# Small comparisons and sums moved from VectorE to GpSimd in an attention kernel, and one early projection moved to another bank

## The chip, the cores and the metric

One core of one Trainium2 chip. The metric is the device time of one execution in microseconds (us), the median of the runs. Below, TensorE is also PE, VectorE is DVE, ScalarE is ACT, GpSimd is POOL, and SyncE, which here only issues transfers, is SP, as in the profile. PEld is TensorE's weight load.

## The reference

The input `x` is 32 images of 256 channels and 32 x 32 pixels, all float32. Each image goes through a group normalisation, 1x1 projections to queries, keys and values (8 heads of 32), causal attention in which a pixel sees only earlier ones, and a residual sum:

```
x = x + conv(_gn(x))
_gn:   g = v.reshape(B, 32, 8, H, W); (g - mean(g)) / sqrt(var(g) + 1e-5)
conv:  q = q_w @ xf + q_b;  k, v = split(kv_w @ xf + kv_b)          # xf: (B, 256, 1024)
       scores = q @ k^T / sqrt(32), masked to tril(-1)
       attn = softmax(scores), 0 where masked;  out = attn @ v
```

## The kernel before

**Visits.** An image is worked through in ten visits: two groups of four heads, five visits each (`VISITS`, lines 638 to 650). In each visit TensorE writes scores of keys against queries, the long pieces into the banks `sT` and the short ones into `tri`; ScalarE takes exponentials without a maximum, of `sT` into `e` (L443, two a visit) and of `tri` into `eh` (L446, three buffers that take turns by visit, line 416); GpSimd sets the masked half of the diagonal blocks to zero (L388, `select`, called by `mask`). One visit later TensorE multiplies the exponentials with the values into the bank `acc` (L472), and VectorE adds the exponentials of different keys up (L490, `add_keys`) for the softmax's denominators.

**Order of the work.** The schedule is written out by hand: nothing is reordered, so that each engine's queue runs in the order in which the loop at line 820 emits. In each turn of that loop the order is: the scores of visit i with their exponentials and selections, the first half of the products of visit i - 1, the list `at[i]`, the second half of those products, `add_keys` of visit i - 1, the list `after[i]`. Work that belongs to other images is hung on visits through `when`: the tuples at lines 720 to 726 (`PROJECT`, `PREPARE`, `SUMS`, `STACK`, `LOAD`, `SPREAD`, `FINISH`) say on which visit, counted from the image's own first visit.

**Normalisation of an image**, eleven to twelve visits ahead of it (`PREPARE`): VectorE's statistics per channel (L196), a transfer out and an indirect transfer back that brings the eight channels of a group together (L205, L212, the latter issued by GpSimd), `norm_groups` (line 217): VectorE aggregates them to mean and variance (L219, twice), and with two small operations on 128x2 numbers makes minus the mean (L222) and the variance plus 1e-5 (L224). One visit later `norm_rstd` (line 248) on GpSimd: the power -0.5 (L250), and `shift`, the product of minus the mean and that (L254). One visit later again, `norm_apply` on ScalarE makes the normalised input `xn` from `x`, `shift` and `rstd` (L269), four operations for each of two halves. Image 0 has its own way through `norm_mean` to `norm_variance`, and its `norm_rstd` does the power alone.

**Denominators.** GpSimd issues transfers that fold the sums over 128 partitions to 32 (L505, `fold`, two a row of sums, each with an accumulation), SP stacks the four rows (L511), and in the next image's visits 5 and 6 VectorE transposes and reduces them (L518, L519, `sum_folded`) into `rows`, 128x64. In visit 7 `invert` (line 550) checks that all sums lie between 1e-20 and 1e20: `check` (line 546) multiplies the tile `in_range` with two comparisons (L547, L548). Then come reciprocal (L554), transpose (L556), a transfer out to DRAM (L559), and transfers back that spread the inverses (L573). `finish` on VectorE multiplies and adds the residual (L598, L601, L606). `in_range` is read once, at the end (line 623), where it decides whether a slower way is taken after all.

**Projections.** `project_qk` (line 271) and `project_v` (line 287) are hung on visits by `PROJECT`. Each writes into a bank that is either `room`, half of one of the `sT` tiles (two projections of the same turn get the two halves of one tile), or `lone`, the bank `acc` of the values' products. For image 0 the first ones run before visit 0: queries of the first half in `lone`, keys of the first half in `room`, the first values `v(0)` in the other half of that tile. ScalarE copies each out (L283, L300). `lone` is used again in visit 0, for the queries of the second half.

## Time and profile before

| | |
|---|---|
| median of 3 runs | 1806.36 us (1802.93 to 1806.63) |
| the profiled execution | 1806.47 us, span 1803.3 us, TensorE's granted clock 0.999 |
| GpSimd's busiest lines | selections L388, transfers L505 |
| chain that ended last | PE 57%, DVE 32%, issue 5%, DMA 3%, ACT 2% |
| in that chain by line | additions L490 20%, products L472 17%, projections L180 14 and 7% |
| TensorE's granted clock | full in all 40 slices |

The busy shares of the page count an engine as busy while an instruction is in flight on it, also when that instruction is stretched by another engine; for TensorE, whose matmuls overlap, a busy engine is not one at its peak. So the share alone does not tell which engine sets the pace. Rows of waits are "engine, line, what it waited for: us in total, times, longest"; rows of a timeline are "start, duration, engine, line, operation, output and inputs, shape, count", with the idle time before in brackets and what ended it. The name in front of the arrow is the tile that is written.

### The profile page before, as it was taken

What the parts mean: (1) busy time and instruction counts of PE and PEld (TensorE: products, weight loads), DVE (VectorE), ACT (ScalarE), POOL (GpSimd) and SP (SyncE); (2) the same over time, 40 slices, a digit from 0 to 9 for tenths busy, and PEclk for the clock granted to TensorE, in tenths of its full rate; (3) what the DMA queues carried; (4) which work ended last, traced back from release to release, by engine and by line L of the source; (5) the groups of instructions that cost most, each with busy time, mean ns of one, the idle gap of its engine ahead of it and who ended that gap; (6) DMA issues with size and microseconds to landing.
All of it is one profiled execution on the core that took longest, in us unless ns stands there. A gap on an engine that the chain in (4) does not pass through costs nothing.

```text
span 1803.3 us, 82014 instructions
## 1 busy us (share of the span) xinstructions
PE 1782.8 (99%) x37208; PEld 983.7 (55%) x37208; DVE 1682.6 (93%) x1852; ACT 1469.8 (82%) x1736; POOL 833.2 (46%) x935
## 2 busy tenths in 40 slices
PE   8999999999999999999999999999999999999998
PEld 5555555555555555555555555555555555555554
DVE  3789999999999999999999999999999999999996
ACT  5888888888888888888888888888888888888884
POOL 2445644444444444544544444545444444445541
PEclk9999999999999999999999999999999999999999
DMA  2566776666766767767667666676676676666662
GB/s 69 105 118 129 150 134 137 137 138 136 149 127 138 144 134 148 129 134 143 131 145 146 129 137 142 137 148 128 136 147 131 145 143 131 138 140 136 131 120 86
DMA packets 92771, 240.23 MB, mean 133 GB/s; under 512 B 26272, under 2 KB 27792, under 8 KB 76544
## 3 DMA queue, kind: packets, MB, share of 16 engines
q0 software_dynamic: 17360, 100.58, 39.0%
q1 hardware_dynamic: 74912, 134.28, 26.3%
q8 instruction: 292, 4.78, 1.1%
q14 instruction: 63, 0.52, 0.1%
q10 hardware_dynamic: 144, 0.07, 0.0%
HBM read 69.90 MB, written 34.95 MB: 58 GB/s over the span
## 4 chain that ended last, share of the span: by engine, by line
PE 57%; DVE 32%; issue 5%; DMA 3%; ACT 2%; DVEq 0%; SPq 0%; POOL 0%; ACTq 0%
DVE e L490 20%; PE acc L472 17%; PE pp L180 14%; PE tri L381 10%; PE sT L381 8%; PE ppv L180 7%; DVE turned L518 3%; DVE rows L519 3%; DVE rb L601 2%; DMA rb<-inverses 2%; DVE num L598 2%; ACT eh L446 2%; DVE st L196 1%; PE pd L526 1%; DVE mv L219 1%
## 5 line engine op out<-in xcount | busy, mean ns | idle before, releaser
L443 ACT ACTIVATE e<-sT 128x1024 f32<-128x1024 f32 x640 | 620.8, 1022 | 209.1 <-PE sT L381 204.3
L381 PE MATMUL tri<-q,k 32*64 32x128 f32 (+4 forms) x12416 | 550.4, 298 | 8.8 <-ACT eh L446 8.1
L381 PE MATMUL sT<-q,k 32*64 32x256 f32 (+1 forms) x7424 | 548.7, 462 | 1.2 <-issue 1.2
L381 PEld LDWEIGHTS tri<-q,k 32*64 32x64 f32 x12416 | 389.0, 131 | 185.9 <-issue 86.6
L388 POOL TENSOR_SCALAR_AFFINE_SELECT diagonal<-eh 128x512 f32<-128x512 f32 x384 | 363.2, 966 | 265.6 <-ACT eh L446 265.3
L180 PE MATMUL pp<-xn,wT 128*32 128x512 f32 (+1 forms) x4224 | 477.5, 582 | 0.0
L490 DVE TENSOR_TENSOR e<-e,eh 128x1536 f32<-128x1536 f32 x375 | 438.3, 1169 | 41.5 <-PE acc L472 28.2
L446 ACT ACTIVATE eh<-tri 128x1536 f32<-128x1536 f32 (+1 forms) x320 | 453.2, 1416 | 23.6 <-DVE e L490 23.6
L490 DVE TENSOR_TENSOR e<-e,e 128x2048 f32<-128x2048 f32 x187 | 447.4, 2393 | 6.4
L505 POOL DMA_DIRECT2D e<-e x248 | 206.5, 833 | 414.9 <-DMA e<-e 360.9
L472 PE MATMUL acc<-e,v 128*32 128x512 f32 x2560 | 338.5, 600 | 1.1 <-POOL diagonal L388 1.1
L381 PEld LDWEIGHTS sT<-q,k 32*64 32x64 f32 x7424 | 301.1, 131 | 15.2 <-issue 1.9
L180 PEld LDWEIGHTS pp<-xn,wT 128*32 128x32 f32 x4224 | 140.5, 109 | 270.6 <-issue 216.2
L490 DVE TENSOR_TENSOR e<-e,diagonal 128x1024 f32<-128x1024 f32 x187 | 245.0, 1310 | 19.4
L180 PE MATMUL ppv<-wT,xn 128*32 128x256 f32 x4032 | 240.6, 379 | 0.0
L472 PE MATMUL acc<-eh,v 128*32 128x384 f32 (+3 forms) x3072 | 198.7, 346 | 0.0
L472 PEld LDWEIGHTS acc<-eh,v 128*32 128x32 f32 x3072 | 97.0, 110 | 143.1 <-issue 120.6
L180 PEld LDWEIGHTS ppv<-wT,xn 128*32 128x32 f32 x4032 | 129.7, 110 | 69.0
L388 POOL TENSOR_SCALAR_AFFINE_SELECT e<-e 128x512 f32<-128x512 f32 x64 | 73.2, 1144 | 196.1 <-ACT e L443 196.1
L269 ACT ACTIVATE xn<-x,shift,rstd 128x256 f32<-128x256 f32 x248 | 135.4, 594 | 8.8 <-POOL shift L254 8.4
L601 DVE SCALAR_TENSOR_TENSOR rb<-num,v_bias_col,x 128x256 f32<-128x256 f32 x248 | 131.3, 569 | 4.4
L472 PEld LDWEIGHTS acc<-e,v 128*32 128x32 f32 x2560 | 62.8, 108 | 105.2 <-issue 94.6
(94 smaller groups left out, 1267.9 us busy)
## 6 DMA issues: line engine op xcount, KB each, us to landing
e<-e POOLq DMA_DIRECT2D x124, 512.0 KB, 6.2
x<-in_x_dram SPq DMA_DIRECT2D x124, 256.0 KB, 4.1
e<-e POOLq DMA_DIRECT2D x124, 256.0 KB, 4.7
folded<-e SPq DMA_DIRECT2D x124, 256.0 KB, 4.5
rb<-inverses SPq DMA_DIRECT2D x124, 256.0 KB, 5.0
out_dram<-rb SPq DMA_DIRECT2D x124, 256.0 KB, 3.8
x<-in_x_dram SPq DMA_DIRECT2D x2, 512.0 KB, 5.8
inverses<-inv_turned SPq DMA_DIRECT2D x31, 32.0 KB, 2.9
```

What stands on the lines that cost most here:

```text
L180: nc.tensor.matmul(out[part, cols], lhsT=lhsT[:, part], rhs=rhs[:, cols], start=start, stop=stop, skip_group_check=True)
L269: nc.scalar.activation(to, of, AF.Identity, bias=live["shift", b][:, g : g + 1], scale=rstd)
L381: return nc.tensor.matmul(to[c : c + KEYS, at : at + width], lhsT=live["k", b, g][rows, kb * P + c : kb * P + c + KEYS], rhs=live["q", b, ...
L388: nc.gpsimd.affine_select(out=to, in_=of, pattern=[[0, 4], [(1, -1)[odd], P]], compare_op=ALU.is_gt, fill=0.0, base=0, channel_multiplier= ...
L443: nc.scalar.activation(e[:, heads[a][0] : heads[a][1] + 1 : step, :], banks[a], AF.Exp)
L446: exp = nc.scalar.activation(eh[:, :, :wide], tri.rearrange("p (j q) -> p j q", q=SHORT)[:, :, :wide], AF.Exp)
L472: nc.tensor.matmul(acc[HD * j : HD * (j + 1), of], lhsT=live["v", b][:, kb, h * HD : (h + 1) * HD], rhs=e[:, j, :], start=first, stop=last ...
L490: nc.vector.tensor_add(to, to, tile_of(b, g, at))
L505: nc.gpsimd.dma_start(out=total[:rows], in_=total[rows : 2 * rows], accum_op=ALU.add)
L518: nc.vector.transpose(turned, live["folded", b][:, j, :])
L519: nc.vector.tensor_reduce(live["rows", b][:, j * HALF // HD : (j + 1) * HALF // HD], turned.rearrange("p (k r) -> p k r", r=HD), AX.X, ALU ...
L601: nc.vector.scalar_tensor_tensor(blocks(rb, s), blocks(num, s, (start + s) % 2 == 1), v_bias_col[:, g : g + 1], blocks(xt[:, g, cols], s), ...
```

## The change

- `norm_groups` ends with the two aggregates; L222 and L224 are gone from VectorE.
- `norm_rstd` on GpSimd, for images 1 to 31, does four operations on 128x2 numbers in place of two: variance plus a tile of 1e-5, power, mean times a tile of -1, that times the power. The two constant tiles are set once at the start.
- `check` runs on GpSimd: each of the two comparisons is a `tensor_scalar` into a tile `held`, and a product of `in_range` with it. It is emitted where it was, ahead of the reciprocal in `invert`.
- For image 0, `v(0)` is put into `lone` instead of `room`.

```diff
+    minus = const.tile([P, NG], F32, name="minus")
+    nc.gpsimd.memset(minus, -1.0)
+    least_variance = const.tile([P, NG], F32, name="least_variance")
+    nc.gpsimd.memset(least_variance, 1e-5)
...
         def norm_groups(b):
             for g in range(NG):
                 nc.vector.bn_aggr(live["mv", b][:, g, :], live["eight", b][:, :, g, :])
-            mv = live["mv", b]
-            live["minus_mean", b] = small.tile([P, NG], F32, tag="mean", name=f"mean_{b}")
-            nc.vector.tensor_scalar(live["minus_mean", b], mv[:, :, 0], -1.0, None, ALU.mult)
-            live["rstd", b] = small.tile([P, NG], F32, tag="rstd", name=f"rstd_{b}")
-            nc.vector.tensor_scalar(live["rstd", b], mv[:, :, 1], 1e-5, None, ALU.add)
...
         def norm_rstd(b):
-            rstd = live["rstd", b]
+            if b == 0:
+                nc.gpsimd.tensor_tensor(live["rstd", b], live["rstd", b], power, ALU.pow)
+                return
+            mv = live["mv", b]
+            rstd = live["rstd", b] = small.tile([P, NG], F32, tag="rstd", name=f"rstd_{b}")
+            shift = live["shift", b] = small.tile([P, NG], F32, tag="shift", name=f"shift_{b}")
+            nc.gpsimd.tensor_tensor(rstd, mv[:, :, 1], least_variance, ALU.add)
             nc.gpsimd.tensor_tensor(rstd, rstd, power, ALU.pow)
-            if b == 0:
-                return
-            live["shift", b] = small.tile([P, NG], F32, tag="shift", name=f"shift_{b}")
-            nc.gpsimd.tensor_tensor(live["shift", b], live["minus_mean", b], rstd, ALU.mult)
+            nc.gpsimd.tensor_tensor(shift, mv[:, :, 0], minus, ALU.mult)
+            nc.gpsimd.tensor_tensor(shift, shift, rstd, ALU.mult)
...
-                qk(0, 0, 0, *early), qk(1, 0, 0), qk(0, 0, 1, *early), v(0), qk(1, 0, 1), qk(0, 1, 0, lone),
+                qk(0, 0, 0, *early), qk(1, 0, 0), qk(0, 0, 1, *early), v(0, *early), qk(1, 0, 1), qk(0, 1, 0, lone),
...
-        def check(rows, least, most):
-            nc.vector.scalar_tensor_tensor(in_range, rows, least, in_range, ALU.is_ge, ALU.mult)
-            nc.vector.scalar_tensor_tensor(in_range, rows, most, in_range, ALU.is_le, ALU.mult)
+        def check(b):
+            for n, (bound, order) in enumerate(((SUM_MIN, ALU.is_ge), (SUM_MAX, ALU.is_le))):
+                held = small.tile([P, ROW], F32, tag="held", name=f"held_{b}_{n}")
+                nc.gpsimd.tensor_scalar(held, live["rows", b], bound, None, order)
+                nc.gpsimd.tensor_tensor(in_range, in_range, held, ALU.mult)
...
-            check(rows, SUM_MIN, SUM_MAX)
+            check(b)
```

## The prediction

> **What bounds the kernel now.** I read the page's busy shares first, then who waited for whom on VectorE (DVE) and on TensorE (PE) over a long steady stretch, then both timelines. The page:
>
> ```profile
> PE 1782.8 (99%) x37208; PEld 983.7 (55%) x37208; DVE 1682.6 (93%) x1852; ACT 1469.8 (82%) x1736; POOL 833.2 (46%) x935
> ```
>
> That reads as a TensorE kernel. The waits from 300 to 1690 us say otherwise. First all those of VectorE, then all those of TensorE:
>
> ```profile
> DVE e L490 <- DVE e L490: 0.5, 1, 0.5
> DVE e L490 <- ACT num L481: 0.5, 1, 0.5
> DVE e L490 <- issue: 0.3, 1, 0.3
> ```
>
> ```profile
> PE tri L381 <- ACT eh L446: 6.6, 15, 0.8
> ```
>
> In 1390 us VectorE waited 1.3 us: it always has something ready. TensorE shows more waiting, and all of it on ScalarE's (ACT's) exponential of the short scores. How much TensorE really loses shows in the time from one image to the next. Visit 5 of images 2, 3 and 30 begins on TensorE at (start, duration, engine, line, shapes):
>
> ```profile
> 159.00 0.56 PE L381 MATMUL tri<-q,k 32*64 32x128 f32 x6
> ```
>
> ```profile
> 213.49 0.56 PE L381 MATMUL tri<-q,k 32*64 32x128 f32 x6
> ```
>
> ```profile
> 1705.54 0.56 PE L381 MATMUL tri<-q,k 32*64 32x128 f32 x6
> ```
>
> Image 2 took 213.49 - 159.00 = 54.49 us; the 27 after it took (1705.54 - 213.49) / 27 = 55.26 us each, with the same matmuls. So 54.49 is TensorE's own pace, 0.77 us an image is lost to something else, and over 27 images that is 20.8 us: the most a relief of VectorE can give in the steady part. A busy TensorE hides it, because a held-up visit also runs its matmuls less tightly.
>
> Where the loss is made, on VectorE's and ScalarE's timelines near the end of image 15:
>
> ```profile
> 894.29 0.69 DVE L519 TENSOR_REDUCE rows<-turned 128x16 f32<-128x512 f32 x1
> 895.01 0.23 DVE L547 SCALAR_TENSOR_TENSOR in_range<-rows,in_range 128x64 f32<-128x64 f32 x1
> 895.27 0.23 DVE L548 SCALAR_TENSOR_TENSOR in_range<-rows,in_range 128x64 f32<-128x64 f32 x1
> 895.41 0.55 DVE L554 RECIPROCAL inv<-rows 128x64 f32<-128x64 f32 x1
> ```
>
> ```profile
> 898.02 1.45 ACT L446 ACTIVATE eh<-tri 128x1536 f32<-128x1536 f32 x1 [0.84 <-DVE e L490]
> ```
>
> After four transposes and four reductions comes the inversion, and behind it, late, the additions of L490 that must free a buffer of `eh`. ScalarE stands 0.84 us for it, and the next visit of TensorE for ScalarE. VectorE, late by up to three buffers, is the bound; TensorE stands 0.77 us an image below it. I argue from VectorE's work per image.
>
> **The change, part by part.** *The check leaves VectorE.* From the start of L547 to that of L554 are 895.41 - 895.01 = 0.40 us, and the sums are there (L519 ends 894.98): 0.40 us an image, right ahead of the additions that ScalarE waits for.
>
> *The two small operations after the aggregate leave VectorE.* Image 16, then image 30:
>
> ```profile
> 921.62 0.62 DVE L222 TENSOR_SCALAR mean<-mv 128x2 f32<-128x2 f32 x1
> 922.14 0.15 DVE L224 TENSOR_SCALAR rstd<-mv 128x2 f32<-128x2 f32 x1
> 922.21 3.00 DVE L490 TENSOR_TENSOR e<-e,eh 128x1536 f32<-128x1536 f32 x2
> ```
>
> ```profile
> 1694.64 0.17 DVE L222 TENSOR_SCALAR mean<-mv 128x2 f32<-128x2 f32 x1
> 1694.72 0.16 DVE L224 TENSOR_SCALAR rstd<-mv 128x2 f32<-128x2 f32 x1
> 1694.85 3.17 DVE L490 TENSOR_TENSOR e<-e,eh 128x1536 f32<-128x1536 f32 x2
> ```
>
> ```profile
> L222 DVE TENSOR_SCALAR mean<-mv x31: 168/295/632, 23.9 to 1694.6; 128x2 f32<-128x2 f32 x31
> ```
>
> They take 922.21 - 921.62 = 0.59 us in one image and 0.21 in the other. The rest, 0.38 us, I read as waiting for GpSimd (POOL), whose mask selections run in the first case; the next addition would meet the same selection, so that part comes back in some measure. I credit 0.28 us, near the lower end with the median of 295 ns in view; the ends are 0.21 and 0.38. Both edits: 0.68 us an image.
>
> *What GpSimd's new work costs VectorE.* Six instructions an image are new on GpSimd: two comparisons and two products of 128x64, an addition and a product of 128x2. The page's groups have one comparison of that size (row L620, its mean in ns), and the trace two cases of GpSimd beside VectorE: the power (alone at 8.90, beside VectorE at 925.57) and the selections of 128x512.
>
> ```profile
> L620 POOL TENSOR_SCALAR rows_last<-inv_last 128x64 f32<-128x64 f32 x1 | 0.4, 403 | 9.8 <-DVE inv_last L587 9.8
> ```
>
> ```profile
> 8.90 0.73 POOL L250 TENSOR_TENSOR rstd<-rstd,power 128x2 f32<-128x2 f32 x1 [6.33 <-DVE rstd L246]
> ```
>
> ```profile
> 925.57 1.56 POOL L250 TENSOR_TENSOR rstd<-rstd,power 128x2 f32<-128x2 f32 x1
> 927.21 0.20 POOL L254 TENSOR_TENSOR shift<-mean,rstd 128x2 f32<-128x2 f32 x1
> ```
>
> ```profile
> 926.45 0.68 DVE L598 TENSOR_TENSOR num<-num,rb 128x512 f32<-128x512 f32 x1
> ```
>
> ```profile
> 1788.50 0.67 DVE L598 TENSOR_TENSOR num<-num,rb 128x512 f32<-128x512 f32 x1
> ```
>
> ```profile
> 898.37 0.80 POOL L505 DMA_DIRECT2D e<-e  x1 [3.46 <-DMA e<-e]
> 899.56 2.29 POOL L388 TENSOR_SCALAR_AFFINE_SELECT diagonal<-eh 128x512 f32<-128x512 f32 x2 [0.39 <-ACT eh L446]
> ```
>
> ```profile
> 901.39 2.60 DVE L490 TENSOR_TENSOR e<-e,e 128x2048 f32<-128x2048 f32 x1
> ```
>
> ```profile
> 929.79 2.29 DVE L490 TENSOR_TENSOR e<-e,e 128x2048 f32<-128x2048 f32 x1
> ```
>
> The power is stretched from 0.73 to 1.56 us and ends with VectorE's product (927.13), which lost 0.01 (0.68 against 0.67). A tiny GpSimd instruction yields. A selection does not: the addition beside it lost 2.60 - 2.29 = 0.31 us. So six instructions cost VectorE between 6 x 0.01 = 0.06 us and, the four larger ones at 0.31 x 0.40 / 1.15 (two selections in 2.29 us) = 0.11 each, 0.45 us. I take 0.1: they are nearer in size to the power, and the first two of the check lie beside the reciprocal and a transpose, which read one operand. Net 0.58 us, so VectorE asks for 55.26 - 0.58 = 54.68 us an image, still 0.19 above TensorE.
>
> [...]
>
> *GpSimd's queue.* The check sits behind visit 7's selections and waits in order for the sums (894.98); four instructions of some 0.4 us end about 896.6. Behind it stands the accumulating transfer that went at 898.37 after 3.46 us of idleness, on another transfer. So it is covered by 1.8 us; uncovered, it would push that transfer and the selections of visit 8.
>
> *The longer chain to the normalised input.* Addition, power and two products now run in turn where power and product did, so `shift` comes later by at least two small instructions (0.4 us), by more if each yields to VectorE. ScalarE already waits for it. Visit 4 and 5 on TensorE with the wait in ScalarE's row, image 16 then image 29:
>
> ```profile
> 927.08 0.56 PE L381 MATMUL tri<-q,k 32*64 32x128 f32 x6
> ```
>
> ```profile
> 927.44 1.09 ACT L269 ACTIVATE xn<-x,shift,rstd 128x256 f32<-128x256 f32 x2 [0.40 <-POOL shift L254]
> ```
>
> ```profile
> 932.36 0.56 PE L381 MATMUL tri<-q,k 32*64 32x128 f32 x6
> ```
>
> ```profile
> 1644.79 0.57 PE L381 MATMUL tri<-q,k 32*64 32x128 f32 x8
> ```
>
> ```profile
> 1646.00 1.09 ACT L269 ACTIVATE xn<-x,shift,rstd 128x256 f32<-128x256 f32 x2 [1.25 <-POOL shift L254]
> ```
>
> ```profile
> 1650.53 0.56 PE L381 MATMUL tri<-q,k 32*64 32x128 f32 x6
> ```
>
> Normalising 0.36 us after the visit's start cost nothing (5.28 us to visit 5); 1.21 after cost 0.46 (5.74). So about 0.4 us of slack is left, and `shift` moves 0.4 to 1.3 us. But the chain's place follows VectorE, which arrives 0.40 + 0.28 us earlier: I book 0, with 0.46 as the other end.
>
> *The first value projection.* It stands at the start, once:
>
> ```profile
> 13.50 0.69 ACT L283 ACTIVATE q<-pp,qk_bias 128x512 f32<-128x512 f32 x1 [1.31 <-PE pp L180]
> 15.21 0.69 ACT L283 ACTIVATE k<-pp,qk_bias 128x512 f32<-128x512 f32 x1 [1.03 <-PE pp L180]
> ```
>
> ```profile
> 15.96 1.93 PE L180 MATMUL pp<-wT,xn 128*32 128x256 f32 x32 [0.80 <-ACT k L283]
> ```
>
> It shares a tile with the key projection and waits 0.80 us for that to be copied out. The values' bank is free since 14.19: 0.8 us gained. The ends are 0 (the start waits for a transfer instead) and 0.8. The two new memsets are hidden ahead of the first load.
>
> **The sum.** 27 x 0.58 = 15.7 us, 0.8 at the start, and 1.0 because VectorE, nearly on TensorE's pace, needs some five more images to fall three buffers behind (5 x 0.19): 17.5 us. The profiled execution took 1806.47 us (span 1803.3), 0.1 over the median of the runs: 1806.47 - 17.5 = 1789.0.
>
> **The rivals.**
> - *TensorE's floor.* The additions meet fewer selections once VectorE is less late, and VectorE drops below 54.49: 20.8 + 0.8 gives 1784.9. For it: the gap is only 0.19. Against: GpSimd has more to do.
> - *`shift` becomes the wait.* If every image pays what image 29 paid, the pace is 54.49 + 0.46 = 54.95: 27 x 0.31 + 0.8 = 9.2 us, 1797.3. For it: ScalarE waits here already. Against: VectorE's head start.
> - *GpSimd takes back what VectorE gave.* At 0.45 us for the new work the net is 0.23 an image: 27 x 0.23 + 0.8 = 7.0 us, 1799.5; at 0.6 no change shows.
> [...]
> - *No relief.* VectorE loses the instructions but waits elsewhere: 1806. Its 1.3 us of waits speak against it.
>
> **Chances.** Forecast 0.52, TensorE's floor 0.18, `shift` 0.14, given back 0.07, no relief 0.03, slower 0.06. Within 0.2% (3.6 us, about what three runs spread over and can tell from no change) lie the last part of "given back" and "no relief": 0.07; slower 0.06; faster 0.87. The range goes from TensorE's floor less the spread of the runs, 1783, to 1800, which takes in `shift`.
>
> **What would show it.** Right: VectorE has four instructions fewer an image; images are 54.5 to 54.8 us apart on TensorE; ScalarE's wait for L490 before `eh` mostly gone; the key-copy wait of 0.80 gone; the check ends before the accumulating transfer. Wrong: the mean durations of L490 rise, ScalarE's wait for `shift` grows several-fold with TensorE waiting behind it, or images stay at 55.2.

## The result and the profile after

The changed kernel took 1857.66 us (median of six runs, 1846.47 to 1865.86), the kernel before 1804.79 on the same chip (1802.93 to 1806.63): ratio 1.0286, interval 1.0242 to 1.0331. The forecast was 1789.0 with 1783 to 1800 as its range, so it was wrong, sign included. The profiled execution took 1853.35 us, span 1850.5, 47.2 us longer than before's span.

Line numbers have moved by three to five: scores are L384, exponentials L446 and L449, additions L493; the four operations to `shift` are L254 to L257, the check L552 and L553, the normalisation L272. The page's busy shares:

```profile
PE 1791.7 (97%) x37208; PEld 988.1 (53%) x37208; DVE 1676.7 (91%) x1728; ACT 1463.4 (79%) x1736; POOL 1021.8 (55%) x1123
```

VectorE has its 124 instructions fewer and is no longer the engine that always has work. Over the same stretch as before, 300 to 1690 us, its longest sum of waits, and TensorE's:

```profile
DVE e L493 <- PE acc L475: 24.4, 15, 3.4
```

```profile
PE ppv L184 <- ACT e L446: 40.7, 20, 3.0
```

VectorE's waits of this stretch were 1.3 us in all before, and TensorE had no such wait. Behind it, on ScalarE, over the whole span:

```profile
ACT xn L272 <- POOL shift L257: 71.9, 27, 4.4
```

That wait was 8.4 us before. Visit 5 of images 15, 16 and 17 begins at:

```profile
901.52 0.56 PE L384 MATMUL tri<-q,k 32*64 32x128 f32 x6
```

```profile
960.44 0.57 PE L384 MATMUL tri<-q,k 32*64 32x128 f32 x6
```

```profile
1014.92 0.56 PE L384 MATMUL tri<-q,k 32*64 32x128 f32 x6
```

One image took 58.92 us, the next 54.48. So the pace of 54.49 that the forecast read as TensorE's own is reached, but only in some images. Image 16, at its visit 4, on GpSimd, VectorE, ScalarE and TensorE in turn:

```profile
949.97 0.69 POOL L254 TENSOR_TENSOR rstd<-mv,least_variance 128x2 f32<-128x2 f32 x1
950.74 0.87 POOL L255 TENSOR_TENSOR rstd<-rstd,power 128x2 f32<-128x2 f32 x1
951.59 0.41 POOL L256 TENSOR_TENSOR shift<-mv,minus 128x2 f32<-128x2 f32 x1
952.08 2.25 POOL L257 TENSOR_TENSOR shift<-shift,rstd 128x2 f32<-128x2 f32 x1
```

```profile
951.00 0.95 DVE L493 TENSOR_TENSOR e<-e,eh 128x768 f32<-128x768 f32 x1
951.99 2.29 DVE L493 TENSOR_TENSOR e<-e,e 128x2048 f32<-128x2048 f32 x1
```

```profile
954.37 1.09 ACT L272 ACTIVATE xn<-x,shift,rstd 128x256 f32<-128x256 f32 x2 [3.44 <-POOL shift L257]
955.36 1.91 ACT L446 ACTIVATE e<-sT 128x1024 f32<-128x1024 f32 x2
```

```profile
956.41 3.54 PE L184 MATMUL ppv<-wT,xn 128*32 128x256 f32 x32 [2.37 <-ACT e L446]
```

Read it from the bottom. TensorE stands 2.37 us for visit 4's exponentials; these are queued on ScalarE behind the normalisation, which stands 3.44 us for `shift`; and `shift` is late because a product of two numbers per partition took 2.25 us. It began 0.09 us after VectorE's addition of 128x2048 and ended 0.05 us after it (952.08 + 2.25 = 954.33 against 951.99 + 2.29 = 954.28). Of the 31 products L257 in the trace, the first two, at the start, take 0.20 and 0.19 us; each of the other 29 ends within 0.08 us behind the end of a VectorE instruction that was running, and 13 of them take 2.25 us, beside that same addition. Where VectorE is idle, in image 0, the four take:

```profile
36.98 0.19 POOL L254 TENSOR_TENSOR rstd<-mv,least_variance 128x2 f32<-128x2 f32 x1
37.25 0.72 POOL L255 TENSOR_TENSOR rstd<-rstd,power 128x2 f32<-128x2 f32 x1
37.96 0.18 POOL L256 TENSOR_TENSOR shift<-mv,minus 128x2 f32<-128x2 f32 x1
38.23 0.20 POOL L257 TENSOR_TENSOR shift<-shift,rstd 128x2 f32<-128x2 f32 x1
```

1.45 us from first to last (38.43 - 36.98); in image 16 it is 4.36. The means of the page's groups (last number ahead of the bar's idle time, in ns), with the check's:

```profile
L552 POOL TENSOR_SCALAR held<-rows 128x64 f32<-128x64 f32 x62 | 57.9, 933 | 2.1
L553 POOL TENSOR_TENSOR in_range<-in_range,held 128x64 f32<-128x64 f32 x62 | 54.7, 883 | 5.2
L257 POOL TENSOR_TENSOR shift<-shift,rstd 128x2 f32<-128x2 f32 x31 | 41.7, 1344 | 2.4
L255 POOL TENSOR_TENSOR rstd<-rstd,power 128x2 f32<-128x2 f32 x31 | 33.4, 1078 | 2.4
```

The power L255 takes 1078 ns in the mean (0.72 us in image 0) and the product L257 1344 (0.20), while the additions of 128x2048 beside the 13 products of 2.25 us take 2.29 each, as in image 16. That is the direction that the forecast did not price: here GpSimd is the one that stands.

The stall costs more than the wait. In the stretches from 954 to 956, 956 to 960 and 960 to 964 us (the clock that TensorE was granted is the last number but two):

```profile
954.00:956.00 2.00, 0.04 (x4) 0.00 (x0) 1.96 (x4) 1.63 (x3) 2.00 (x3) 1.00 0.46 130
956.00:960.00 4.00, 3.58 (x44) 1.79 (x48) 3.83 (x5) 2.61 (x3) 0.98 (x2) 0.57 0.95 199
960.00:964.00 4.00, 4.00 (x84) 2.17 (x76) 3.86 (x3) 3.57 (x6) 0.00 (x0) 1.00 0.55 163
```

From 956.32 us, 0.09 us ahead of the end of the idle time, TensorE is granted 0.50 of its clock for 3.41 us (0.50 in the stretch from 956.40 to 959.70), and the projection takes 3.54 us where it takes 1.93 in the prediction's row of the same 32 matmuls. That happened in eight images, for 3.41 us in each.

What a late `shift` costs can be read image by image. Where the first normalisation begins up to 0.54 us behind visit 4's start on TensorE, visit 4 takes its shortest time, 5.28 us. From 1.52 us on it loses that delay less 0.8 us (1.52 gives 0.71, 2.05 gives 1.24, 4.07 gives 3.25), and 1.0 to 1.7 us more in the eight images with half clock: in image 16 a delay of 3.41 us (954.37 against 950.96) costs 4.20.

**Where the 47.2 us are.** I take the start of each visit on TensorE and the shortest time of each of the ten visits in images 2 to 30 as its floor. Image 0 begins 1.28 us earlier (16.54 against 17.82), images 0 and 1 are together 1.13 shorter, images 2 to 30 together 49.6 longer. Within these 49.6: visit 4 lost 62.8 us over its floor (2.4 before), visit 1 6.4 (0.65), visit 5 1.6 (0.03), while the loss in visits 8 and 9 went from 18.2 to 0.1. The ten floors add up to 54.48 us before and 54.47 after.

### The profile page after: what moved, and what is told of

It is laid out like the page before. It is cut to its first block, busy times and chain, and to the rows that moved or that the text cites. A ratio compares the mean times of both kernels' runs of the same rounds, so it can differ in the third digit from the quotient of the medians.

```text
span 1850.5 us, 82078 instructions
## 1 busy us (share of the span) xinstructions
PE 1791.7 (97%) x37208; PEld 988.1 (53%) x37208; DVE 1676.7 (91%) x1728; ACT 1463.4 (79%) x1736; POOL 1021.8 (55%) x1123
## 4 chain that ended last, share of the span: by engine, by line
PE 56%; DVE 15%; POOL 9%; issue 7%; DMA 6%; ACT 5%; POOLq 1%; DVEq 0%; ACTq 0%; SPq 0%
PE acc L475 16%; PE pp L184 15%; DVE e L493 9%; PE tri L384 8%; PE ppv L184 8%; PE sT L384 8%; DMA e<-e 3%; POOL diagonal L391 3%; ACT e L446 2%; DMA eight<-each,group_of 2%; DVE num L603 2%; DVE rb L606 2%; POOL held L552 1%; ACT xn L272 1%; ACT eh L449 1%
## 5 line engine op out<-in xcount | busy, mean ns | idle before, releaser
L446 ACT ACTIVATE e<-sT 128x1024 f32<-128x1024 f32 x640 | 620.1, 1021 | 228.7 <-PE sT L384 215.9
L384 PE MATMUL sT<-q,k 32*64 32x256 f32 (+1 forms) x7424 | 549.1, 462 | 0.5 <-issue 0.5
L384 PE MATMUL tri<-q,k 32*64 32x128 f32 (+4 forms) x12416 | 542.2, 298 | 0.9 <-ACT eh L449 0.9
L493 DVE TENSOR_TENSOR e<-e,eh 128x1536 f32<-128x1536 f32 x375 | 431.9, 1152 | 69.1 <-PE acc L475 55.7
L391 POOL TENSOR_SCALAR_AFFINE_SELECT diagonal<-eh 128x512 f32<-128x512 f32 x384 | 353.8, 958 | 245.1 <-ACT eh L449 244.8
L384 PEld LDWEIGHTS tri<-q,k 32*64 32x64 f32 x12416 | 388.2, 131 | 173.7 <-issue 77.0
L493 DVE TENSOR_TENSOR e<-e,e 128x2048 f32<-128x2048 f32 x187 | 456.5, 2441 | 6.4
L449 ACT ACTIVATE eh<-tri 128x1536 f32<-128x1536 f32 (+1 forms) x320 | 453.0, 1416 | 0.0
L508 POOL DMA_DIRECT2D e<-e x248 | 216.7, 874 | 347.1 <-DMA e<-e 236.2
L384 PEld LDWEIGHTS sT<-q,k 32*64 32x64 f32 x7424 | 302.2, 131 | 14.0 <-issue 1.6
L184 PE MATMUL ppv<-wT,xn 128*32 128x256 f32 x4064 | 252.9, 391 | 44.1 <-ACT e L446 44.1
L493 DVE TENSOR_TENSOR e<-e,diagonal 128x1024 f32<-128x1024 f32 x187 | 250.3, 1339 | 19.4
L272 ACT ACTIVATE xn<-x,shift,rstd 128x256 f32<-128x256 f32 x248 | 135.6, 597 | 72.0 <-POOL shift L257 71.9
L391 POOL TENSOR_SCALAR_AFFINE_SELECT e<-e 128x512 f32<-128x512 f32 x64 | 79.5, 1242 | 178.0 <-ACT e L446 178.0
L606 DVE SCALAR_TENSOR_TENSOR rb<-num,v_bias_col,x 128x256 f32<-128x256 f32 x248 | 135.1, 585 | 4.4
L603 DVE TENSOR_TENSOR num<-num,rb 128x512 f32<-128x512 f32 x124 | 102.5, 827 | 25.0 <-DMA rb<-inverses 22.9
```

The costliest lines, as they stand in the source:

```text
L184: nc.tensor.matmul(out[part, cols], lhsT=lhsT[:, part], rhs=rhs[:, cols], start=start, stop=stop, skip_group_check=True)
L272: nc.scalar.activation(to, of, AF.Identity, bias=live["shift", b][:, g : g + 1], scale=rstd)
L384: return nc.tensor.matmul(to[c : c + KEYS, at : at + width], lhsT=live["k", b, g][rows, kb * P + c : kb * P + c + KEYS], rhs=live["q", b, ...
L391: nc.gpsimd.affine_select(out=to, in_=of, pattern=[[0, 4], [(1, -1)[odd], P]], compare_op=ALU.is_gt, fill=0.0, base=0, channel_multiplier= ...
L446: nc.scalar.activation(e[:, heads[a][0] : heads[a][1] + 1 : step, :], banks[a], AF.Exp)
L449: exp = nc.scalar.activation(eh[:, :, :wide], tri.rearrange("p (j q) -> p j q", q=SHORT)[:, :, :wide], AF.Exp)
```

## The experiments

Every kernel was timed beside the kernel before on the same chip; its ratio to that is given with the interval. "Chain" is from the start of the first of GpSimd's small operations to the end of `shift`'s product.

**The parts alone.** First the four operations on GpSimd alone (check and bank as before):

```diff
-            nc.vector.tensor_scalar(live["minus_mean", b], mv[:, :, 0], -1.0, None, ALU.mult)
-            nc.vector.tensor_scalar(live["rstd", b], mv[:, :, 1], 1e-5, None, ALU.add)
...
+            nc.gpsimd.tensor_tensor(rstd, mv[:, :, 1], least_variance, ALU.add)
             nc.gpsimd.tensor_tensor(rstd, rstd, power, ALU.pow)
...
-            nc.gpsimd.tensor_tensor(live["shift", b], live["minus_mean", b], rstd, ALU.mult)
+            nc.gpsimd.tensor_tensor(shift, mv[:, :, 0], minus, ALU.mult)
+            nc.gpsimd.tensor_tensor(shift, shift, rstd, ALU.mult)
```

> The change's normalisation part alone: the four operations on 128x2 numbers on GpSimd; the check stays on VectorE, the first value projection where it was. Theory (the chain: each small GpSimd operation waits for the VectorE instruction that runs, shift comes late, ScalarE stands in front of the exponentials of visit 4, TensorE behind it): slower than before by 25 to 65 us, visit 4 taking up to 10 us, ScalarE waiting 50 us or more for shift. Rival 1 (the check on GpSimd delays the folding transfers): about as before, 1795 to 1806. Rival 2 (GpSimd's instructions slow VectorE down as a whole): 5 to 15 us slower, spread over all visits.

1829.94 us, ratio 1.0109 (1.0086 to 1.0132). ScalarE's wait for `shift`:

```profile
ACT xn L272 <- POOL shift L257: 58.7, 26, 4.3
```

Visit 4 lost 44.9 us in the profiled execution (1835.68, the longest of the four), visits 8 and 9 1.1. This part alone makes the kernel slower, in the place that the theory names. The check alone, its comparisons and products on GpSimd as in the change:

```diff
-            check(rows, SUM_MIN, SUM_MAX)
+            check(b)
```

> The check on GpSimd alone, everything else as before. Theory: faster, 1788 to 1798, since 0.40 us an image leave VectorE and GpSimd has room in visit 7; the waits of ScalarE for L490 before eh shrink, ScalarE's wait for shift stays near 8 us. Rival 1 (the check is what hurts): slower by 20 us or more. Rival 2 (GpSimd slows VectorE down): 1803 to 1815.

1804.28 us, ratio 0.9981 (0.9971 to 0.9990): a small gain, below what the theory expected. Visits 8 and 9 lost 8.5 us (18.2 before), but visits 1, 2 and 4 lost 9.6 (3.1 before). VectorE did not keep its relief either. The selections that stand behind the check come later, and in one image both of them now fall on the same long addition:

```profile
901.99 1.49 POOL L388 TENSOR_SCALAR_AFFINE_SELECT diagonal<-eh 128x512 f32<-128x512 f32 x2
```

```profile
902.10 3.54 DVE L490 TENSOR_TENSOR e<-e,e 128x2048 f32<-128x2048 f32 x1
```

This addition, the fourth of its size in an image, took 2.60 us in the prediction's row and takes 3.37 in the mean here. Over the whole trace the instructions that VectorE kept took 8.7 us more than before, 0.28 us an image, though some of the shorter additions became faster. The bank alone:

```diff
-                qk(0, 0, 0, *early), qk(1, 0, 0), qk(0, 0, 1, *early), v(0), qk(1, 0, 1), qk(0, 1, 0, lone),
+                qk(0, 0, 0, *early), qk(1, 0, 0), qk(0, 0, 1, *early), v(0, *early), qk(1, 0, 1), qk(0, 1, 0, lone),
```

> The first value projection in the values' bank alone. Theory: 0.8 to 1.3 us faster at the start and nothing else, within 0.2%. Rival 3 (the earlier start puts the whole kernel in another phase, and that is what the change lost by): slower by 10 us or more.

1806.04 us, ratio 0.9993 (0.9983 to 1.0002); the first visit begins 0.83 us earlier. And the change without the bank:

```diff
-                qk(0, 0, 0, *early), qk(1, 0, 0), qk(0, 0, 1, *early), v(0, *early), qk(1, 0, 1), qk(0, 1, 0, lone),
+                qk(0, 0, 0, *early), qk(1, 0, 0), qk(0, 0, 1, *early), v(0), qk(1, 0, 1), qk(0, 1, 0, lone),
```

> The changed kernel without the move of the first value projection's bank: norm steps and check on GpSimd. The normalisation alone took 1829.9 us and the check alone 1804.3, against 1857.7 for the whole change; bank alone was 0.9993. Theory (the check's four GpSimd operations make the folds and the norm chain later, on top of the longer chain; the bank counts for nothing after image 0): 1840 to 1862 us, ScalarE's wait for `shift` 60 to 80 us. Rival 1 (the effects add, 22 and -3): 1822 to 1832 us, and then the bank move is what makes the rest. Rival 2 (the starting phase decides which images fall in the stall, so that the bank's 1.3 us moves the whole): anything from 1815 to 1870 us with the stalls in other images than in the changed kernel.

1851.26 us, ratio 1.0265 (1.0221 to 1.0309), with 66.9 us of waiting for `shift`: the bank counts for nothing here, and norm and check together are more than their sum.

**Is it the late `shift`?** The changed kernel with the first normalisation one visit later, so that its `xn` no longer stands ahead of visit 4's exponentials:

```diff
-        PREPARE = (-12, -11, -10, -10, -9, -8, -7, -6, -4, -4, -3)
+        PREPARE = (-12, -11, -10, -10, -9, -8, -6, -6, -4, -4, -3)
-                prepare(1, (None, None, None, None, 1, 2, 3, 4, 6, 6, 7))
+                prepare(1, (None, None, None, None, 1, 2, 4, 4, 6, 6, 7))
```

> The changed kernel, with the first of ScalarE's normalisations (L272, first half, first group) hung one visit later, on visit 4 in place of 3, ahead of nothing that needs it sooner. GpSimd's and VectorE's work is that of the changed kernel. Theory: shift has one visit more, the wait for it and the stalls of visit 4 go, and what is left is TensorE's own pace: 1780 to 1788. Rivals 1 and 2 (the check's delay, or VectorE slowed down): it stays above 1830, or above 1800.

1809.93 us, ratio 1.0011 (0.9980 to 1.0042), the executions from 1793.6 to 1818.6. The expected median was missed, but 48 us of the loss went with nothing changed on GpSimd or VectorE: in the profiled execution (1793.6) visit 4 lost 1.8 us. So the loss is what stands behind the late `shift`; the spread is taken up below.

**Is it the reading, or the number of operations?** The kernel before, VectorE untouched, with two operations more on GpSimd between power and `shift`. In one kernel they are products that nobody reads, as here; in the other they are fills, with `nc.gpsimd.memset(idle, 0.25)` as the last line.

```diff
+            for n in range(2):
+                idle = small.tile([P, NG], F32, tag="idle", name=f"idle_{b}_{n}")
+                nc.gpsimd.tensor_tensor(idle, power, power, ALU.mult)
```

> The kernel before, with VectorE's work untouched, and two idle 128x2 products (`power` times `power` into a tile that nobody reads) on GpSimd between the power and `shift`'s product: GpSimd's part of the chain to `shift` has four small operations, as in the changed kernel. Theory (each small GpSimd operation that reads SBUF is held until the running VectorE instruction ends; in the changed kernel the four take 3 to 5.6 us against 1.44 us alone): the two products add 1 to 3 us to the chain, ScalarE's wait for `shift` grows from 8.4 us to 40 us or more, and the time is 1820 to 1850 us. Rival 1 (the order of the chain, with variance and minus mean no longer made by VectorE ahead of time, is what hurts, not the count of GpSimd's operations): 1803 to 1810 us. Rival 2 (operations that nobody waits for by their result don't delay the next one): the same 1803 to 1810 us, with `shift`'s product starting within 0.5 us of the power's end.

1817.81 us, ratio 1.0061 (1.0043 to 1.0079).

```profile
L255 POOL TENSOR_TENSOR idle<-power 128x2 f32<-128x2 f32 x62 | 17.0, 319 | 0.0
L257 POOL TENSOR_TENSOR shift<-mean,rstd 128x2 f32<-128x2 f32 x31 | 12.9, 416 | 0.0
```

> As the run with two idle products, but the two idle operations are fills of 128x2 with a constant: they write SBUF and read none. Theory (what is held is a read of SBUF by GpSimd against VectorE's two-input instructions): each fill takes some 0.2 us, the chain grows by 0.4 us, and the time is 1804 to 1814 us, at least 10 us below the run with products. Rival 1 (anything small on GpSimd is held while VectorE runs, reads or not): as the products, 1820 to 1850 us. Rival 2 (the count of operations costs nothing, see the products): both 1803 to 1810 us.

1807.08 us, ratio 1.0000 (0.9990 to 1.0010).

```profile
L255 POOL MEMSET idle<- 128x2 f32 x62 | 7.6, 209 | 0.0
L257 POOL TENSOR_TENSOR shift<-mean,rstd 128x2 f32<-128x2 f32 x31 | 6.5, 209 | 0.0
```

Two fills cost nothing: 52 of the 62 took 0.09 us, as the fills at the program's start do (0.10), and the other ten began while the power ahead of them was under way and ended within 0.1 us behind it. Two products that read SBUF are held in part (17 of 62 took over 0.3 us, up to 1.75), double the time of the product behind them, and cost 0.6%. In this pair the operations that read are held and the ones that only write are not. How the 0.6% comes about is another matter. In the profiled execution images 2 to 30 took 9.1 us more than before; visit 4 accounts for 2.6 of these and visits 8 and 9, where TensorE stands behind VectorE, for 5.5. On VectorE the `rb<-num` instructions of `finish` took 148.6 us in place of 141.2, so VectorE's time was touched as well. And the products were held less than I had expected: 0.32 us each, where the additions and products of the changed kernel's chain have means of 0.64 to 1.34; the time stayed under the expected range. I then thought that an operation which depends on nothing slips in before VectorE's next instruction starts, and tried the reverse, two products that each need the one ahead:

```diff
+            same = rstd
+            for n in range(2):
...
+                nc.gpsimd.tensor_tensor(kept, same, one, ALU.mult)
+                same = kept
```

> The kernel before with two 128x2 products by one on GpSimd between the power and `shift`'s product, each on the result of the one ahead, where the run with idle products had two that depend on nothing (1817.8 us, means of 0.32 us each and 0.42 us for `shift`'s product). VectorE's work is untouched. Theory as it now stands (an operation that depends on the one ahead starts some 0.08 us after it, when the next VectorE instruction has begun, and is held to that instruction's end; one that depends on nothing starts before the one ahead ends and slips in): each of the three products behind the power takes 0.5 to 1.4 us in the mean, the chain from the power to `shift` 3.5 to 5 us against 2.2, and the time is 1822 to 1850 us. Rival (only the number of operations counts, not what they depend on): 0.3 to 0.45 us each and 1813 to 1820 us, as with the idle ones.

1821.18 us, ratio 1.0074 (1.0055 to 1.0093), which overlaps the run with idle products: the time doesn't tell them apart. In the profiled execution (1835.95, the longest of the four) the means were 0.32, 0.80 and 1.09 us and the chain 4.7 us in the median, against 2.2 with idle products. Two kernels for the order of the four, on the changed kernel:

```diff
             nc.gpsimd.tensor_tensor(rstd, mv[:, :, 1], least_variance, ALU.add)
-            nc.gpsimd.tensor_tensor(rstd, rstd, power, ALU.pow)
             nc.gpsimd.tensor_tensor(shift, mv[:, :, 0], minus, ALU.mult)
+            nc.gpsimd.tensor_tensor(rstd, rstd, power, ALU.pow)
             nc.gpsimd.tensor_tensor(shift, shift, rstd, ALU.mult)
```

> The changed kernel with the four operations in the order variance plus bound, minus mean, power, product: the minus mean depends on nothing ahead of it, the product still follows the power at once. Theory: the minus mean slips in at 0.2 to 0.4 us (0.64 in the changed kernel), the power stays at 0.75 to 1.1 us, the product stays held at 1.0 to 1.4 us; the chain is 3.0 to 3.8 us long against 4.3, and the time 1820 to 1845 us, 15 us or more below the changed kernel and above before. Rival (the order is nothing, each of the four meets one VectorE instruction): 1847 to 1866 us.

1804.32 us, ratio 0.9998 (0.9978 to 1.0018), 53 us under the changed kernel and more than I had expected: exchanging two lines that do not depend on each other. One image of it:

```profile
480.54 0.65 POOL L254 TENSOR_TENSOR rstd<-mv,least_variance 128x2 f32<-128x2 f32 x1
481.17 0.18 POOL L255 TENSOR_TENSOR shift<-mv,minus 128x2 f32<-128x2 f32 x1
481.31 0.94 POOL L256 TENSOR_TENSOR rstd<-rstd,power 128x2 f32<-128x2 f32 x1
482.34 0.71 POOL L257 TENSOR_TENSOR shift<-shift,rstd 128x2 f32<-128x2 f32 x1
```

```profile
482.04 0.95 DVE L493 TENSOR_TENSOR e<-e,eh 128x768 f32<-128x768 f32 x1
483.02 2.75 DVE L493 TENSOR_TENSOR e<-e,e 128x2048 f32<-128x2048 f32 x1
```

The product by -1 follows the addition without a gap (481.17 against 481.19), so one wait fewer is met; the last product is held by the addition of 128x768, to 483.05, and not by the long one of 128x2048 that comes next, as in the changed kernel. With an idle product put between power and last product, it should have slipped in better still:

```diff
+            idle = small.tile([P, NG], F32, tag="idle", name=f"idle_{b}")
+            nc.gpsimd.tensor_tensor(idle, power, power, ALU.mult)
             nc.gpsimd.tensor_tensor(shift, shift, rstd, ALU.mult)
```

> The reordered kernel with a fifth, idle 128x2 product between the power and `shift`'s product; it depends on nothing. Theory (the idle product slips in behind the power, the product behind it too, so that five operations take less than four): the idle product takes 0.2 to 0.4 us, `shift`'s product 0.2 to 0.5 us in place of 1.34, the chain 2.2 to 3.0 us, and the time is 1793 to 1815 us, below the reordered kernel by 15 us or more. Rival (more operations on GpSimd are more holds): the same as the reordered kernel or above it, 1830 to 1870 us.

1835.65 us, ratio 1.0156 (1.0133 to 1.0178): the expectation failed, in the direction of its rival. The idle product took 0.59 us and the last one 0.61; in most images one more held operation was met. So "what depends on nothing slips in" is no rule. What holds in all of these traces is simpler: of GpSimd's 1178 additions and products of 128x2 all but one end within 0.21 us behind the end of a VectorE instruction or start between two (from 0.04 us ahead of the one's end to 0.1 us behind the other's start). In these kernels one more of them was one more VectorE instruction to sit out, unless it happened to catch the gap. Where the end of the chain falls (its median over images 2 to 29, from the start of visit 3 on TensorE, which lasts 5.31 us) goes, roughly, with what visit 4 loses (sum over images 2 to 30; all from the one profiled execution of each kernel):

| kernel | chain, us | end after visit 3's start, us | visit 4 loses, us |
|---|---|---|---|
| before | 1.7 | 5.6 | 2.4 |
| two fills | 1.7 | 5.6 | 5.1 |
| two idle products | 2.2 | 6.0 | 5.0 |
| reordered | 2.4 | 6.2 | 10.8 |
| interleaved | 3.0 | 6.9 | 27.9 |
| norm alone | 4.4 | 7.3 | 44.9 |
| without bank | 4.1 | 7.4 | 53.5 |
| chained products | 4.7 | 7.4 | 44.6 |
| changed | 4.3 | 8.2 | 62.8 |

(A median of start and one of length need not add up to that of the end.)

**Without the chain.** Variance plus bound and minus the mean on ScalarE, `shift` by two ScalarE operations just ahead of the normalisation; GpSimd keeps the power, the check and, for the start, the bank move stays:

```diff
+            nc.scalar.activation(rstd, mv[:, :, 1], AF.Identity, bias=eps)
+            nc.scalar.activation(mean, mv[:, :, 0], AF.Identity, scale=-1.0)
             nc.gpsimd.tensor_tensor(rstd, rstd, power, ALU.pow)
...
+            nc.scalar.activation(shift[:, g : g + 1], mean[:, g : g + 1], AF.Identity, scale=rstd[:, g : g + 1])
```

> The changed kernel with only the power left to GpSimd: variance plus bound and minus mean are made by ScalarE right behind the aggregate, and `shift` by two 128x1 ScalarE operations just ahead of the normalisation. Check on GpSimd and bank move stay. Theory (what hurt was the chain of four held GpSimd reads; VectorE's relief is real and leaves TensorE's 54.48 us per image as the pace): the stall of visit 4 goes, ScalarE's wait for GpSimd falls below 15 us, and the time is 1783 to 1798 us. Rival 1 (ScalarE's added operations, four of 0.2 to 0.3 us per image in a stretch where TensorE waits for its exponentials, become the wait): 1800 to 1815 us, with TensorE waiting for ScalarE in visits 2 to 4. Rival 2 (the check on GpSimd is what delays folds and chain): above 1815 us.

1793.98 us, ratio 0.9921 (0.9903 to 0.9939): the fastest of all, below both kernels. The chain is one operation, visit 4 loses 3.9 us, visits 8 and 9 5.0. VectorE's relief is real once nothing is paid for it: 0.79% is some 14 us, and images 2 to 30 took 9.6 us less in the profiled execution. The same with the check back on VectorE:

```diff
-            check(b)
+            check(rows, SUM_MIN, SUM_MAX)
```

> The kernel with variance and minus mean on ScalarE (1794.0 us, ratio 0.9921), with the check left on VectorE as in the kernel before. Theory (the check alone was worth 0.9981; VectorE, with the two small operations gone, is near TensorE's pace, so that 0.3 us per image of check still shows for a part): 1794 to 1802 us, with 3 to 8 us more lost in visits 8 and 9 than the 5.0 us there. Rival (the check's four GpSimd operations, 1.0 and 0.6 us each, hold up selections and folds; without them the loss of 3.9 us in visit 4 and 2.1 us in visit 3 goes): 1784 to 1792 us.

1799.62 us, ratio 0.9962 (0.9950 to 0.9974): 12.5 us lost in visits 8 and 9. With a short chain the check on GpSimd is a gain of some 0.4%. And with the first normalisation one visit later (image 1's list too, as above):

```diff
-        PREPARE = (-12, -11, -10, -10, -9, -8, -7, -6, -4, -4, -3)
+        PREPARE = (-12, -11, -10, -10, -9, -8, -6, -6, -4, -4, -3)
```

> The kernel with variance and minus mean on ScalarE (1794.0 us, with 3.9 us of its images 2 to 30 still lost in visit 4, 2.1 in visit 3 and 5.0 in visits 8 and 9), with the first normalisation of xn taken one visit later. Theory (what visit 4 still loses is the late `shift`; the later place covers it): 1786 to 1793 us. Rival (the later place brings new stalls in visits 7 to 9, as one execution of the changed kernel with the later place showed, and scatter: 1793.6 to 1818.6 us): 1794 to 1815 us.

1821.09 us, ratio 1.0094 (1.0065 to 1.0123). The theory fell. In visit 5 of one image ScalarE now runs without any idle time ahead of the exponentials:

```profile
943.90 0.30 ACT L261 ACTIVATE shift<-mean,rstd 128x1 f32<-128x1 f32 x1
944.23 1.09 ACT L280 ACTIVATE xn<-x,shift,rstd 128x256 f32<-128x256 f32 x2
945.22 0.28 ACT L261 ACTIVATE shift<-mean,rstd 128x1 f32<-128x1 f32 x1
945.53 1.10 ACT L280 ACTIVATE xn<-x,shift,rstd 128x256 f32<-128x256 f32 x2
946.53 1.91 ACT L454 ACTIVATE e<-sT 128x1024 f32<-128x1024 f32 x2
```

Two normalisations with their small operations in one visit, 2.6 us, put the exponentials late, and visit 5 takes at least 6.30 us where it takes 5.72: 0.58 us in each image, 17 us in 29. Another 13.6 us went in visit 1, in eight images, which the rival had not named; no run shows what made that.

**The spread.** The executions of the changed kernel with the later place lie within 25.0 us, those of the reordered kernel within 18.3, where the runs of the kernel before beside them spread over 4.2 and 6.7. With both, that is the reordered kernel and

```diff
-        PREPARE = (-12, -11, -10, -10, -9, -8, -7, -6, -4, -4, -3)
+        PREPARE = (-12, -11, -10, -10, -9, -8, -6, -6, -4, -4, -3)
```

> The reordered kernel (1804.3 us, 1797.6 to 1816.0; its profiled execution of 1797.7 still loses 10.8 us in visit 4, with the end of `shift`'s product at 6.2 us after visit 3's start in the median) with the first normalisation of xn one visit later. Theory (both its loss and its scatter come from the visits in which the chain to `shift` meets a long VectorE instruction; with the short chain the later place covers it always): 1784 to 1797 us, all executions within 10 us. Rival (the later place brings its own loss, as with the normalisation on ScalarE, 1821.1 us, where visit 5 took 6.30 us in place of 5.73 in every image): 1797 to 1820 us, visit 5 longer or stalls in visit 1. Rival 2 (the scatter of some 20 us has nothing to do with the chain): the lowest near 1790, the highest above 1805.

1804.81 us, ratio 0.9984 (0.9962 to 1.0005), from 1792.65 to 1813.38: the chain alone does not make the spread. The profiled execution loses 7.7 us in visit 1. On GpSimd ahead of one of these:

```profile
176.97 0.80 POOL L552 TENSOR_SCALAR held<-rows 128x64 f32<-128x64 f32 x1
177.85 1.19 POOL L553 TENSOR_TENSOR in_range<-in_range,held 128x64 f32<-128x64 f32 x1
179.11 0.98 POOL L552 TENSOR_SCALAR held<-rows 128x64 f32<-128x64 f32 x1
180.18 2.19 POOL L553 TENSOR_TENSOR in_range<-in_range,held 128x64 f32<-128x64 f32 x1
183.71 0.85 POOL L508 DMA_DIRECT2D e<-e  x1 [1.34 <-issue]
...
192.85 0.78 POOL L508 DMA_DIRECT2D e<-e  x1 [6.20 <-DMA e<-e]
193.39 2.04 POOL L391 TENSOR_SCALAR_AFFINE_SELECT e<-e 128x512 f32<-128x512 f32 x1
```

The check takes 5.4 us (182.37 - 176.97), the fold's transfer is issued behind it, the next fold waits for those transfers, and the selection that TensorE needs in visit 1 stands behind both. So the reordered kernel, and the one with both, each with the check on VectorE:

```diff
-            check(b)
+            check(rows, SUM_MIN, SUM_MAX)
```

> The reordered kernel (1804.3 us, 1797.6 to 1816.0 in ten executions) with the check left on VectorE. Theory (the check's four GpSimd operations, 5.9 us from first to last in one image of the reordered kernel with the later place, hold up the folds' issues behind them, so that the chain to `shift` and the selections of visit 1 come late in some images and not in others; that makes the scatter): all executions within 8 us, 1793 to 1803 us, visit 1 loses under 1 us in all. Rival (the scatter is made by the chain to `shift` alone, whose length depends on the VectorE instructions that it meets): 1797 to 1815 us, spread over 12 us or more as with the check on GpSimd.

> The same with the first normalisation of xn one visit later (1804.8 us with the check on GpSimd, 1792.7 to 1813.4, 7.7 us lost in visit 1 of its profiled execution). Theory (check makes the scatter): 1788 to 1799 us, all within 8 us, visit 1 under 1 us. Rival (later place or chain makes it): spread over 12 us or more, highest above 1806.

1805.38 us (1801.37 to 1809.06), ratio 0.9998 (0.9989 to 1.0007), and 1803.73 us (1799.32 to 1809.44), ratio 0.9986 (0.9975 to 0.9996). Visit 1 loses nothing any more (under 0.1 us), and the spreads are 7.7 and 10.1 us where they were 18.3 and 20.7, with ten to twelve executions of each. The check on GpSimd makes about half of the spread and, in the second kernel, all of visit 1's loss; the rest of the spread is left open. Both medians are above what I had expected, and the second kernel missed the 8 us as well.

**Why norm and check are more than their sum.** From visit 3's start, GpSimd's chain begins at 2.8 us with the norm alone, and at 3.8 and 3.9 with the check too (without bank and changed). The fold's transfer stands behind the check's four operations, and the folds behind it, each waiting for the one ahead, pass the delay on to the chain. But this is a reading, and the record limits it. The reordered kernel begins its chain at 4.0 us with the check on GpSimd and at 3.9 with it on VectorE, and the kernel before, without either part, at 3.7. The profiled executions of norm alone and of the change without bank differ by 13.6 us, the medians by 21.3. Why the two parts are more than their sum stays open.

## Why the prediction was wrong, by its steps

- *What bounds the kernel*: right. VectorE was the bound, and 54.49 us is TensorE's own pace: the floors of the ten visits add up to it. How much the relief gives can't be read from the changed kernel. Its visits 8 and 9 lost 0.1 us in place of 18.2, but with chained products, where VectorE keeps all its work, they lost only 3.1: I read that as the stalls of visit 4 letting VectorE catch up. Without that stall (variance and mean on ScalarE) they lost 5.0, and the kernel gained some 14 us where the sum has 17.5.
- *The check leaves VectorE*, 0.40 us an image: too high for what arrived. Alone the check gave 0.19% (about 3 us), since its cost came back in visits 1, 2 and 4 and in a longer addition on VectorE; with a short chain it gave 0.4% (0.9962 to 0.9921), some 7 us or 0.25 an image.
- *GpSimd's new work costs VectorE 0.1 us*: right for the small instructions themselves, too low in all. The 13 additions beside a product of 2.25 us took 2.29 each, as the undisturbed one at 929.79 before, so that "a tiny GpSimd instruction yields" was the right reading. What the term leaves out is that the instructions push the selections behind them onto other additions: with the check alone the rest of VectorE's work grew by 0.28 us an image, in the changed kernel by 0.55 (17.1 us over 31), the pushed selections and all else together. The reciprocal, which the term counts on, shows in one image of the changed kernel with the later place: a comparison of 128x64 took 0.39 us (at 228.81) beside the reciprocal's 0.55 (at 228.74), and the next comparison, beside an addition, 1.82. In the changed kernel's own profiled execution none of the check's 124 operations ran beside an inversion.
- *The longer chain*: this is the step that failed. The prediction had `shift` coming "later by at least two small instructions (0.4 us), by more if each yields to VectorE", let it move 0.4 to 1.3 us, and booked 0 with 0.46 an image as the other end. The row that it quoted itself, the power at 1.56 us in place of 0.73, showed what yielding costs the one that yields: the power began 0.26 us after an addition of 128x1024 (925.31) and stood. The row was used for VectorE's account alone. The chain grew from 1.7 to 4.3 us, its end moved by 2.6, and visit 4 lost 60 us more than before, or 2.1 us in each of 29 images. "The chain's place follows VectorE" did not help: the chain began at 3.9 us after visit 3's start, against 3.7 before.
- *What a late `shift` costs*: the rival had the mechanism, "`shift` becomes the wait", with 0.14, but its price of 0.46 us an image came from a delay of 1.21 us, the longest of the kernel before; the changed kernel's went to 4.33. The slack was 0.8 us and not 0.4, as the same image shows (1.21 less 0.46). The rival did not follow the wait to TensorE's clock, which in eight images added 1.0 to 1.7 us.
- *GpSimd's queue*, "covered by 1.8 us" with "four instructions of some 0.4 us": wrong. The check's operations took 0.93 and 0.88 us in the mean, 3.6 us in all, and the cover went: visit 1 lost 6.4 us, which the norm alone does not lose (0.02).
- *The first value projection*: 0.8 us booked, and the first visit began 0.83 us earlier with the move alone (1.28 in the changed kernel); in the time of the whole kernel it cannot be told from no change.
- *A slower kernel* had a chance of 0.06. Where GpSimd's product and VectorE's long addition met, it was GpSimd that stood: beside the 13 products of 2.25 us the addition took its 2.29. That the time went up as this chance had it was luck.

## What to carry to other kernels

When small operations move to GpSimd beside a VectorE that is always busy, here with additions and products of two tiles, count each as one whole VectorE instruction of latency (0.2 us alone, up to 2.25 here), not as its own length, and ask who waits for the last of them. The chain of them was as long as the run of VectorE instructions it happened to meet (four took 4.3 us in the median, 2.4 in another order): shorten it, or give it to an engine that is not held (here ScalarE, whose 62 operations on 128x1 took 294 ns in the mean; 1794 us), before looking at what the bound engine gains. An operation that frees the bound engine pays only if what it feeds has slack for the new latency, and that slack (0.8 us here) is read from the consumer's waits in the profile of before, from an image that lost as well as from one that did not.

## What the runs showed of the hardware that was not expected

- An addition or product of 128x2 on GpSimd, which reads SBUF, took 0.18 to 0.20 us with VectorE idle and up to 2.25 us beside an addition of 128x2048; a fill of the same size took 0.09 us in 52 of 62 cases with VectorE just as busy.
- The one that waits cost the other nothing measurable: VectorE's long addition took 2.29 us beside each of the 13 products that it held for 2.25. A selection of 128x512 is another matter: beside two of them the same addition took 3.54 us (check alone).
- Eight idle times of TensorE of 2.26 to 2.94 us were followed by 3.41 us at a granted clock of 0.50, so that in image 16 a wait of 2.37 us cost 4.20. Five idle times of 2.33 to 3.04 us passed without it, in other images. The eight stretches begin at 212.22, 324.86, 440.91, 498.94, 669.60, 956.32, 1126.99 and 1243.04 us, which are 33, 34, 17, 50, 84, 50 and 34 times 3.413 us apart; 3.412 to 3.413 us is also the length of each in the trace. With the execution cut into steps of that length at these starts, the step just ahead of each stretch holds 2.11 to 2.56 us of idle TensorE, and no other step of the steady part more than 1.99: each of the five waits without half clock lay across the border of two steps.
- Exchanging two independent small operations moved the median of the whole kernel by 53 us, from 1857.66 to 1804.32.
